# A new table of due times for the software-pipelined period of a two-layer graph network on one core

## The chip, the core and the metric

The kernel runs on one core of one Trainium2 chip. The metric is the device time of one launch in microseconds (us). The kernel before took 772.05 us as the median of three runs (771.89 to 772.5). Names of engines: PE is the matrix engine (its weight loads are shown apart as PEld), DVE the vector engine, ACT the scalar engine, POOL the general engine, SP the engine whose queue issues most DMAs.

## What is computed

There are 128 graphs of 128 nodes with 64 features. An edge exists where `adj > 0`. Two layers follow each other, each with a residual and a layer norm:

```python
# layer 0, F = 64, H = 192
mask = adj > 0
h   = relu((x @ W1a)[:, :, None, :] + (x[:, :, None, :] - x[:, None, :, :]) @ W1b + b1)
hm  = einsum('bjkh,bjk->bjh', h, mask)
x   = layernorm(x + hm @ W2 + deg[..., None] * b2)
# layer 1, H = 128, out 64
agg = einsum('bmn,bnd->bmd', adj, x)
x   = layernorm(x + elu(elu(agg @ V1 + c1) @ V2 + c2) @ V3 + c3)
```

The costly part is `hm`: for each edge a vector of 192 is formed, rectified and summed over the neighbours of a node.

## The kernel before

The graphs are worked off in 64 pairs. For one pair p the steps are these, with the line on which their PE instructions stand:

- `prepare`: DVE makes the mask and the degrees (L545), POOL copies the degrees (L552, L553), PE spreads them over the partitions (step "spread", three products, issued by `stationary` on L246 or L248), DVE ranks the nodes by degree (L568) and builds the permutation (L575).
- `sort_mask`: PE sorts the mask and turns the permutation round (step "sort", four products through `stationary`), ACT copies the results (mtp L659, permT L661), PE forms the prefix sums (step "prefix", one product of 256 columns through `stationary`), ACT copies them (vp L668), DVE builds nine one-hot tables (oh, L675).
- `sort_x` and `project_a`: PE sorts x (L592), ACT copies it (xsT L596), PE multiplies by the weights (step "proja", L606), ACT adds the bias (aj, L613), POOL and DVE form a correction (L620, the PE step "short" on L626 and L629, L635, L642).
- `turn` and `project_c`: PE transposes adj and x (L690, L691), ACT copies them (turned, L695), PE multiplies by the weights (step "projc", L708 and L711), ACT, DVE and POOL split the product into three bf16 parts (L718, L722, L725, L727).
- nine `unit`s: for a block of nodes ACT fills a PSUM bank with aj (L910), PE adds the gathered neighbours by 18 matmuls over the one-hot table (L920), DVE sums absolute values (L930). The blocks have 162, 66, 168, 112, 168, 154, 169, 154 and 170 columns.
- `finish`: POOL subtracts the correction (L842), PE projects (step "proj", L847 and L851), ACT copies (ys, L855), PE unsorts (L864), then the norm, PE aggregates (step "agg", L871), ACT copies (agg, L875), PE, ACT and DVE make the two hidden layers (steps "hid1" L880, "hid2" L886; elu on L791, L794, L797), PE makes the last layer (step "last", L891 and L893), then the norm and the store.

PE holds its array in one of three shapes: whole (128 rows by 128 columns), in two halves of 64 columns (the units, "short", sortx L592, "agg"), and in two halves of 64 rows (L708). `stationary` (L242 to L248) issues a product in two instructions of 64 columns each when the array stands in column halves at that point of the plan, and in one instruction of 128 columns otherwise.

The order of everything is written out at build time. The class `Flow` keeps a model clock for each engine and a list of threads, one for each of the pieces above. A thread yields its next step with an engine, a cost in us and the events that it needs. The table `DUE` gives each step of each thread a time relative to `ROUND * p`, with `ROUND = 11.1651`. While `under_way` is set, which holds from the first unit until 14 units before the last, `run` takes from the steps whose events are already planned the one with the smallest due time, whatever its readiness:

```python
            if self.under_way:
                t, th = min(ready, key=lambda r: self._rank(r[1]))
```

So in the middle of the run the order within one period, on every engine, is what `DUE` says. The costs and `CHANGE`, the model's charge for leaving a PE shape, enter the times at which the model believes a bank or a value to be free, and the choice before the first unit and in the last 14. Four PSUM banks, m0 to m3, serve all steps but the units, which have four of their own, e0 to e3; a step that needs a bank takes the one that heads the list of freed banks (`self.free.pop(0)`), so the order of the steps also decides which bank each uses, and with it for whose copy it waits.

Of the kernel before, what the change touches and what calls it, by code (L numbers as in the profile page):

```python
# [47 lines left out]
def gnn_kernel(ctx: ExitStack, tc: tile.TileContext, x, adj, w1, b1, w2, b2,  # L48
# [28 lines left out]
    with ExitStack() as fast:  # L77
        loads = fast.enter_context(tc.tile_pool(name="loads", bufs=8))
        prep = fast.enter_context(tc.tile_pool(name="prep", bufs=5))
        work = fast.enter_context(tc.tile_pool(name="work", bufs=5))  # L80
        ps_e = fast.enter_context(tc.tile_pool(name="ps_e", bufs=1, space=bass.MemoryType.PSUM))
        ps_m = fast.enter_context(tc.tile_pool(name="ps_m", bufs=1, space=bass.MemoryType.PSUM))
        K = sparse(tc, locals())
# [103 lines left out]
def sparse(tc, env):  # L187
# [15 lines left out]
    AHEAD = 4  # L203

    DUE = {
        "prepare": (-42.67, -37.79, -37.67, -37.41, -37.15),
        "sort_x": (-21.11, -18.03, -15.85, -13.03, -12.9, 2.76, 2.89, 3.02, 3.14),
        "sort_mask": (-28.04, -27.66, -27.27, -15.21, -14.95, -14.31, -14.05, -13.8, -13.54,
                      -13.28, -3.02, -2.76, -2.5, -2.25),
        "turn": (-38.05, -37.92),  # L210
        "project_c": (-31.63, -29.71, -29.58, -29.45, -29.32, -17.13, -13.15),
        "finish": (12.51, 20.73, 21.24, 21.37, 21.5, 21.88, 22.01, 27.91, 28.3, 28.68, 32.02,
                   34.97, 35.1, 35.23, 41.26, 41.39, 43.95, 44.08, 46.78, 46.91, 54.48, 54.61,
                   59.48),
        "unit": [(0.06, 0.19, 0.32), (0.83, 0.96, 1.09), (0.45, 0.58, 0.71), (2.37, 2.5, 2.63),
                 (3.27, 3.4, 3.53), (4.43, 4.56, 4.68), (4.81, 4.94, 5.07), (5.33, 5.71, 6.1),
                 (7.64, 10.97, 11.1)],
    }

    def begin_thread(name, p, gen):  # L220
# [958 lines left out]
```

## Time and profile before

| | |
|---|---|
| median of three runs | 772.05 us |
| the profiled execution's own time | 772.32 us |
| its span, first to last instruction | 770.6 us |
| PE busy | 746.3 us, 97% of the span |
| DVE, ACT, POOL busy | 725.2, 705.5, 430.1 us |
| mean granted PE clock | 0.985 |
| chain that ended last, by engine | PE 94%, DVE 3%, ACT 2% |
| one period (start of L847 to the next start of L847 in the middle of the run) | 11.39 us |

Times in the profile are us unless marked ns. A row of a group names the line, the engine, the operation, the tile written and the tiles read, the shapes and the number of instructions, then the busy time, the mean ns of one, and the idle time of the engine before them with what ended it. A row of the timeline gives start, duration, engine and line; idle time before it stands in brackets. Matmuls are pipelined, so their durations overlap, and a PE that is busy all the time isn't therefore at its peak: what a step costs is read from the distance between its start and the next step's start. A float32 product stands as two matmuls and two weight loads in the trace.

### The profile page before, as it was taken

To read this page: it belongs to the slowest core of one execution; us is meant where nothing else is said; L and a number is where in the kernel's file an instruction comes from. 1 tells how busy PE (TensorE), PEld (TensorE's weight loads), DVE (VectorE), ACT (ScalarE), POOL (GpSimd) and SP (SyncE) were. 2 spreads that over 40 slices of the span, in tenths; PEclk is the share of its full clock that TensorE was granted. 3 is DMA by queue.
4 is the path that set the end of the run, shared out by engine and by line. 5 is a ranking of instruction groups with operands and counts; after the bars stand their busy time and mean duration, and the time that the engine had idled before them with its cause. 6 is when DMAs were issued, how large, how long until landed. Compare 5 with 4: busy or idle time off the path is not lost.

```text
span 770.6 us, 36007 instructions
## 1 busy us (share of the span) xinstructions
PE 746.3 (97%) x14616; PEld 679.5 (88%) x14617; DVE 725.2 (94%) x2381; ACT 705.5 (92%) x1986; POOL 430.1 (56%) x801
## 2 busy tenths in 40 slices
PE   7599999999999999999999999999999999999995
PEld 5489999999999999999999999999999999999993
DVE  6699999999999999999999999999999999999994
ACT  5479999999999999999999999999999999999984
POOL 5145565565565565556556556556555655655652
PEclk9699999999999999999999999999999999999997
DMA  4000010110110011011011011011101101100000
GB/s 123 11 3 3 17 30 17 30 31 20 27 30 23 24 31 30 16 31 30 17 30 30 17 30 31 21 26 31 30 17 30 31 16 31 31 17 19 11 10 21
DMA packets 54668, 19.70 MB, mean 26 GB/s; under 512 B 37601, under 2 KB 54497, under 8 KB 54497
## 3 DMA queue, kind: packets, MB, share of 16 engines
q1 hardware_dynamic: 53792, 17.05, 9.1%
q8 instruction: 116, 1.90, 1.0%
q14 instruction: 56, 0.45, 0.2%
q10 hardware_dynamic: 704, 0.30, 0.2%
HBM read 13.14 MB, written 4.19 MB: 22 GB/s over the span
## 4 chain that ended last, share of the span: by engine, by line
PE 94%; DVE 3%; ACT 2%; issue 0%; DMA 0%; POOL 0%; ACTq 0%; POOLq 0%; DVEq 0%
PE e L920 45%; PE m L606 6%; PE m L708 5%; PE m L847 5%; PE m L880 4%; PE m L886 4%; PE m L864 4%; PE m L893 4%; PE m L690 3%; PE m L248 2%; PE m L871 2%; PE m L592 2%; PE m L246 2%; PE m L851 1%; PE m L711 1%; PE m L691 1%
## 5 line engine op out<-in xcount | busy, mean ns | idle before, releaser
L920 PE MATMUL e<-oh,cp 128*64 128x162 bf16 (+3 forms) x10368 | 392.7, 229 | 6.2 <-DVE oh L675 5.2
L920 PEld LDWEIGHTS <-cp 128*64 128x64 bf16 x10368 | 356.9, 110 | 15.3 <-issue 6.9
L930 DVE TENSOR_REDUCE sums<-e 128x54 f32<-128x486 f32 (+8 forms) x576 | 327.1, 609 | 16.7 <-PE m L629 9.9
L910 ACT COPY e<-aj 128x504 f32<-128x504 f32 (+6 forms) x576 | 293.3, 540 | 9.5 <-DVE sums L930 8.9
L749 POOL TENSOR_SCALAR ve<-st 128x2 f32<-128x2 f32 x126 | 24.1, 191 | 254.1 <-DVE st L742 246.9
L675 DVE TENSOR_TENSOR oh<-vp,slotc 128x308 bf16<-128x308 bf16 (+6 forms) x576 | 137.3, 314 | 0.8 <-ACT vp L668 0.6
L750 POOL TENSOR_TENSOR rs<-ve,mhalf 128x2 f32<-128x2 f32 x126 | 87.8, 696 | 10.5
L727 POOL TENSOR_TENSOR cp<-r,cp 128x512 bf16<-128x512 f32 x64 | 74.4, 1162 | 18.6 <-ACT cp L725 18.6
L642 POOL TENSOR_TENSOR corr<-ea,sa 128x384 f32<-128x384 f32 x64 | 64.2, 1003 | 32.8 <-DVE ea L635 32.8
L842 POOL TENSOR_TENSOR hm<-sums,corr 128x384 f32<-128x384 f32 x63 | 63.1, 1002 | 5.8 <-DVE sums L930 5.8
L620 POOL TENSOR_TENSOR sa<-aj,srow 128x384 f32<-128x384 f32 x64 | 65.4, 1021 | 0.0
L797 DVE SCALAR_TENSOR_TENSOR h<-m,cc,e 128x256 f32<-128x256 f32 x128 | 60.8, 475 | 3.8 <-ACT e L794 3.6
L791 ACT ACTIVATE r<-m,cc 128x256 f32<-128x256 f32 x128 | 61.3, 479 | 2.4 <-PE m L886 2.4
L606 PEld LDWEIGHTS m<-xsT,wad 128*128 128x128 f32 x384 | 48.3, 193 | 13.0 <-ACT turned L695 11.8
L613 ACT ACTIVATE aj<-m,b1c 128x128 f32<-128x128 f32 x192 | 57.2, 386 | 2.3 <-PE m L606 2.3
L606 PE MATMUL m<-xsT,wad 128*128 128x128 f32 x384 | 58.4, 289 | 0.6 <-DVE r L722 0.6
L794 ACT ACTIVATE e<-r 128x256 f32<-128x256 f32 x128 | 53.3, 418 | 2.0
L847 PE MATMUL m<-w2d,hm 128*128 128x128 f32 x384 | 53.4, 276 | 0.0
L722 DVE TENSOR_TENSOR r<-m,cp 128x256 f32<-128x256 f32 x128 | 47.8, 415 | 2.8 <-ACT cp L718 2.8
L771 ACT ACTIVATE x<-y,nb,rs 128x64 f32<-128x64 f32 x126 | 48.9, 439 | 1.4 <-POOL nb L753 1.4
L847 PEld LDWEIGHTS m<-w2d,hm 128*128 128x128 f32 x384 | 48.1, 192 | 0.1
L708 PE MATMUL m<-wc,turned 64*128 64x256 f32 x256 | 46.3, 436 | 0.9 <-DVE r L722 0.9
(159 smaller groups left out, 1350.5 us busy)
## 6 DMA issues: line engine op xcount, KB each, us to landing
adj<-in_adj_dram SPq DMA_DIRECT2D x64, 128.0 KB, 2.4
xx<-in_x_dram SPq DMA_DIRECT2D x64, 64.0 KB, 2.2
out_dram<-o SPq DMA_DIRECT2D x64, 64.0 KB, 1.6
w1s<-in_L_gnn_W_dram ACTq DMA_DIRECT2D x2, 96.0 KB, 2.8
w2s<-in_L_gnn_W_dram ACTq DMA_DIRECT2D x2, 48.0 KB, 2.7
v2s<-in_L_gnn_W_dram SPq DMA_DIRECT2D x1, 64.0 KB, 2.3
v1d<-in_L_gnn_W_dram SPq DMA_DIRECT2D x2, 32.0 KB, 2.0
rows<-in_L_gnn_b_dram SPq DMA_DIRECT2D x1, 64.0 KB, 4.8
```

Of the source, the lines that this page charges most:

```text
L606: nc.tensor.matmul(aps[:, c * N:(c + 1) * N], wad[:, c, :], xsT, start=True, stop=True)
L620: evs, = yield ("POOL PORT", 1.0, [have] + made("srow"), 0, lambda: nc.gpsimd.tensor_mul(sa, aj, srow))
L642: ev, = yield ("POOL PORT", 1.05, [ev, evs], 0, lambda: nc.gpsimd.tensor_sub(corr, ea, sa))
L675: lambda: nc.vector.tensor_tensor(oh[:, :, c].rearrange("p b (s w) -> p b s w", w=w), vp[:, :, p0:p1].rearrange("p b (o w) -> p b o w", o= ...
L708: nc.tensor.matmul(cps[s][:, :cols], d["turned"][k, 2, :], wc[k, :], start=True, stop=False)
L727: lambda: nc.gpsimd.tensor_sub(cp[:, 2], r1, cp[:, 1]))
L750: nc.gpsimd.tensor_tensor(rs, ve, mhalf, op=OP.pow)
L842: lambda: (nc.vector if late else nc.gpsimd).tensor_sub(hm, d["sums"], d["corr"]))
L847: nc.tensor.matmul(yb[:, :2 * O], hm[:, c, :], flat(w2d[:, c]), start=(c == 0), stop=False)
L910: lambda: nc.scalar.copy(e.rearrange("p (c s w) -> p c s w", c=3, w=w), d["aj"][:, :, p0:p1].rearrange("p c (o w) -> p c o w", o=1) .to_br ...
L920: nc.tensor.matmul(e[s * HB:(s + 1) * HB, c * n:(c + 1) * n], cp[:, k, s, c * HB:(c + 1) * HB], oh[:, s, base:base + n], start=False, stop ...
L930: nc.vector.tensor_reduce(d["sums"][:, :, p0:p1], e.rearrange("p (c s w) -> p c w s", c=3, w=w), AX.X, OP.add, apply_absolute_value=True)
```

## The change

Only the table `DUE` changes; every step, its cost in the plan, `ROUND`, `CHANGE`, the pools and the banks stay as they are. The new due times come from a plan in which leaving a PE step for another kind of matmul was charged by its time in a trace; that plan isn't part of the kernel, only its table is.

```diff
     DUE = {
-        "prepare": (-42.67, -37.79, -37.67, -37.41, -37.15),
-        "sort_x": (-21.11, -18.03, -15.85, -13.03, -12.9, 2.76, 2.89, 3.02, 3.14),
-        "sort_mask": (-28.04, -27.66, -27.27, -15.21, -14.95, -14.31, -14.05, -13.8, -13.54,
-                      -13.28, -3.02, -2.76, -2.5, -2.25),
-        "turn": (-38.05, -37.92),
-        "project_c": (-31.63, -29.71, -29.58, -29.45, -29.32, -17.13, -13.15),
-        "finish": (12.51, 20.73, 21.24, 21.37, 21.5, 21.88, 22.01, 27.91, 28.3, 28.68, 32.02,
-                   34.97, 35.1, 35.23, 41.26, 41.39, 43.95, 44.08, 46.78, 46.91, 54.48, 54.61,
-                   59.48),
-        "unit": [(0.06, 0.19, 0.32), (0.83, 0.96, 1.09), (0.45, 0.58, 0.71), (2.37, 2.5, 2.63),
-                 (3.27, 3.4, 3.53), (4.43, 4.56, 4.68), (4.81, 4.94, 5.07), (5.33, 5.71, 6.1),
-                 (7.64, 10.97, 11.1)],
+        "prepare": (-43.06, -42.93, -39.21, -39.08, -35.87),
+        "sort_x": (-26.76, -10.46, -10.33, -3.14, -3.02, 2.5, 2.63, 2.76, 2.89),
+        "sort_mask": (-26.12, -25.99, -25.86, -23.42, -23.29, -23.16, -13.67, -13.28, -13.03,
+                      -12.77, -2.63, -2.25, -1.99, -1.73),
+        "turn": (-36.9, -36.77),
+        "project_c": (-32.15, -29.32, -29.2, -29.07, -28.94, -4.17, -4.04),
+        "finish": (12.64, 19.44, 19.57, 21.62, 21.75, 21.88, 22.01, 28.04, 28.17, 29.2, 33.56,
+                   33.69, 33.82, 34.71, 43.31, 43.44, 44.47, 44.6, 46.52, 46.65, 48.06, 48.19,
+                   59.87),
+        "unit": [(-1.48, 0.96, 1.09), (2.12, 2.25, 2.37), (3.02, 3.14, 3.27), (3.66, 3.79, 3.91),
+                 (4.68, 4.81, 4.94), (5.07, 5.2, 5.33), (5.97, 6.1, 6.22), (6.35, 6.48, 6.61),
+                 (7.25, 11.61, 11.74)],
     }
```

What it makes of the order was read from the two built programs. The number of instructions on DVE, ACT, POOL and SP is the same, and SP's order is the same. On PE the number of products is the same, but more of them are issued in two halves: 842 matmuls on L246 in place of 498, and 91 on L248 in place of 263. One period on PE in the middle of the run, from "proj" on, with the units by their columns, the bank in brackets, and the array's shape ahead of each stretch:

```
before
whole    proj(m2) hid1(m1) unsort(m3)
columns  170 162 168 66
rows     projc(m2,m3)
whole    last(m0)
columns  112 short(m1) 168 sortx(m0) 154 169 sort(m1) 154 agg(m2)
whole    turn(m3) spread(m1) prefix(m2) hid2(m0) proja(m3)

after
whole    proj(m2) hid2(m0) prefix(m3) unsort(m2) hid1(m1)
columns  170 sortx(m3) 162
rows     projc(m2,m0)
whole    last(m3)
columns  66 short(m1) 168 112 168 154 spread(m3) agg(m1) 169 154 sort(m2)
whole    turn(m0) proja(m1)
```

On ACT, within a period, the copy of turned (L695) is followed at once by aj, ys and the fill of a unit, and not by vp; xsT (L596) follows the elu of both layers and not the copy of agg. On DVE the ranks (L568) stand between two sums over units, and the permutation (L575) among the one-hot tables and not ahead of them. On POOL sa (L620) follows the small degree copies (L552, L553), and the two norms stand apart.

## Prediction

> **What bounds the kernel now.** I read the page first, then the span cut into its stages, then one period instruction by instruction.
>
> ```profile
> PE 746.3 (97%) x14616; PEld 679.5 (88%) x14617; DVE 725.2 (94%) x2381; ACT 705.5 (92%) x1986; POOL 430.1 (56%) x801
> PEclk9699999999999999999999999999999999999997
> ```
>
> The stretches of the span (length, then busy us of PE, PEld, DVE, ACT, POOL, granted clock):
>
> ```profile
> 25.40:50.60 25.20, 17.84 (x363) 15.92 (x363) 20.39 (x68) 15.16 (x41) 5.58 (x8) 0.83 0.01 3
> 72.10:721.10 649.00, 649.00 (x12993) 595.40 (x12992) 630.23 (x2046) 625.11 (x1765) 376.35 (x680) 1.00 0.10 25
> 721.10:770.60 49.50, 40.09 (x711) 35.86 (x709) 37.03 (x118) 34.27 (x96) 23.20 (x42) 0.90 0.06 14
> ```
>
> From 72.1 to 721.1 PE is never idle: 57 equal periods of 649.0/57 = 11.386 us, 84% of the span. So the period is a sum of PE steps, each from its start to the next one's start. But a wait can hide in this: a matmul's recorded duration runs on while its weights are still missing. Such waits show as a first pass that is longer than its sisters. The timeline around the whole-array steps:
>
> ```profile
> 389.44 0.14 PEld L691 LDWEIGHTS m<-ident,xx 128*128 128x128 f32 x1
> 389.56 0.27 ACT L596 COPY xsT<-m 128x128 f32<-128x128 f32 x1
> 389.77 0.10 PEld L248 LDWEIGHTS <-prefix 128*128 128x128 bf16 x1
> 389.82 0.27 PE L248 MATMUL m<-mtp,prefix 128*128 128x256 bf16 x1
> 389.86 0.48 ACT L695 COPY turned<-m 128x384 f32<-128x384 f32 x1
> 389.88 0.30 PEld L886 LDWEIGHTS m<-h,v2s 128*128 128x128 f32 x2
> 389.93 0.43 PE L886 MATMUL m<-h,v2s 128*128 128x256 f32 x1
> 390.20 0.38 PE L886 MATMUL m<-h,v2s 128*128 128x256 f32 x1
> 390.38 0.30 PEld L606 LDWEIGHTS m<-xsT,wad 128*128 128x128 f32 x2 [0.21 <-ACT turned L695]
> 390.42 0.35 PE L606 MATMUL m<-xsT,wad 128*128 128x128 f32 x1
> ...
> 392.00 0.36 PE L880 MATMUL m<-agg,v1p 128*128 128x128 f32 x1
> 392.20 0.27 ACT L855 COPY ys<-m 128x128 f32<-128x128 f32 x1
> 392.53 0.32 PE L864 MATMUL m<-ys,permT 128*128 128x64 f32 x1
> ```
>
> Three loads come just after an ACT copy ends: L886 (hid2, bank m0) at 389.88, after xsT has left m0 at 389.83; L606 (proja, m3) at 390.38, after turned has left m3 at 390.34; L864 (unsort) 0.05 after ys is there. Their first passes take 432, 346 and 315 ns where later ones take 378, 275 and 276:
>
> ```profile
> L886 PE MATMUL m<-h,v2s x128: 378/432/797, 70.9 to 761.7; 128*128 128x256 f32 x128
> L606 PE MATMUL m<-xsT,wad x384: 274/275/527, 15.0 to 731.0; 128*128 128x128 f32 x192
> ```
>
> The excess is 54 + 71 + 39 = 164 ns in each period, in which PE is counted busy. A cross-check without the wait is the early round whose L606 starts right behind "prefix": 49.90 to L847 at 50.56, 0.67 us, against 390.42 to 391.16, 0.74 us.
>
> **What the Trainium skill says.** "TensorE: Matmul & The Clock Gate", section "LDWEIGHTS (loading the stationary operand)", prices a load by its columns, 128/1.2 = 107 ns as an estimate; float32 loads here follow each other by 0.11 us, which agrees. Its table at the top says that loads are pulled ahead of running matmuls; L606 at 49.79 beside "prefix" agrees, and a load that waits for a bank (above) loses just this. "TensorEngine Tiling (Array Packing)", "Key Properties", says that changing the tiling mode drains the engine: "agg" (column halves) starts at 388.94, its passes need 0.22, and turn (whole) starts at 389.27, so the drain costs 0.1 us. Part 1 of the first page says that the clock halves when PE is idle; the 6 in the second slice of PEclk agrees.
>
> **The change, part by part.**
>
> *Switches of shape.* A period before has whole, columns, rows, whole, columns, whole: five. After it has the same five. At 0.1 us each this is neither gain nor loss; only the neighbours change (rows after 162 and not 66, whole after the bf16 "sort" and not after "agg").
>
> *Spread in halves.* Before, three whole products take 389.66 to 389.82 = 0.17 us. After, six half products: "sort" has eight of the same size in 388.09 to 388.31 = 0.22, so 6 x 0.028 = 0.17. Nothing.
>
> *The whole-array steps.* Before, from "prefix" on: prefix 0.11, hid2 0.49, proja 0.74, proj 0.84, hid1 0.53, unsort 0.58 (with the drain) = 3.29. After: proja behind turn, in bank m1 and so not waiting for the copy of turned: 6 x 0.112 = 0.67. proj 0.84. hid2 now follows the 64-column bf16 passes of proj, which hide only 0.03 of its 0.11 load: that exposure is what hid1 shows today (356 against 275 ns), 0.08; 0.08 + 2 x 0.215 = 0.51. prefix 0.11, and its 256 columns hide unsort's load. unsort 4 x 0.112 = 0.45. hid1 3 x 0.112 + 0.205 with the drain = 0.54. Sum 3.12. The difference, 0.165 us, is the same as the three waits: the exposure behind proj only changes its owner. 57 periods x 0.165 = 9.4 us.
>
> *What becomes late next.* unsort still needs ys: today it comes 0.55 us after proj's last pass, and in between stand hid2's 0.51 and a bit, so its margin is about nil; I take no loss, at worst 0.05. proj takes bank m2 from sort, so it waits for permT: the copies end 1.1 us after sort starts (388.09 to 389.21), and turn and proja give it 0.22 + 0.15 + 0.38 + 0.67 = 1.4 us; the margin of 0.3 is used up if ACT is at the fill of a unit (0.53) when sort ends: from nothing to 0.2 lost, I take nothing. prefix now waits for vp and a bank behind hid2, with mtp made 1.5 us ahead. On DVE, nine one-hots, nine sums and the rest need 13.5 us of durations in a period, of which back-to-back ones overlap by 0.08 (nine one-hots of mean 0.314 take 2.14 us together): 32 instructions, so 10.9 us. In a period of 11.22 this leaves 0.3. ACT and POOL have more. SP's order is the same, loads land periods ahead of use.
>
> *The start.* Before the first unit the order also changes. Today the first unit stands from 25.76 to 30.68 behind DVE's chain of constants (L508 at 24.14 to L366 at 28.7) and nine one-hots (2.15 us); the chain starts when PE has run L504 and L505, which stand behind two runs of projc. In the new order one of these runs comes after L505, but the split of its product (L722, two of 0.41) stands inside the chain. I work out L504 some 2.5 us sooner, of which the wait for that projc (at half clock 1.8 us, and copies) takes half back: 1.2 gained. Between 30.68 and 50.56 PE also idles: 1.17 (DVE r), 0.56, 0.42 and 0.29 before units, more inside L606. The new order puts the second pair's projc and sortx elsewhere; I take 1.8 of it as saved. So 3.0, bounds 0 and 5.5 (the upper one with the full clock coming back sooner; it is 0.83 on average in that stretch).
>
> *The end.* The last store was due 59.48 after its period's start and is due 59.87; the last 14 units run in a free order in both. I take 0, bounds -1.5 and +1.5.
>
> Sum against the profiled execution: 772.3 - 9.4 - 3.0 = 759.9; the median of the runs is 0.3 below that execution, so **759.6 us**.
>
> **The rivals.**
>
> *A, the forecast:* the three waits go, nothing takes their place, the start is shorter. 756 to 763 us.
>
> *B, the waits change places:* permT before proj, or ys before unsort, or the fill of a unit. For it speaks that the new margins are 0 to 0.3 us. With 0.1 lost per period, 57 x 0.1 = 5.7: 765 us, range 763 to 770.
>
> *C, DVE becomes the bound:* its need is 10.9 us and it is idle 0.5 today. If its new order leaves the same idle time, the period stays at 11.39; with no gain at the start either, 772. Against it: what it waits for today is mostly PE, which comes sooner.
>
> *D, slower:* the elu behind hid2. projc takes bank m0 from hid2, so it waits for h2 (L797). From hid2's last pass (390.20) to the end of h2 takes 3.85 us today (the same step a period earlier: r at 379.63, e at 380.97, h at 382.18 to 382.65). After, PE reaches projc's load 0.22 + 0.11 + 0.45 + 0.54 + 0.69 + 0.22 + 0.73 = 2.96 later. If ACT and DVE took as long as now, each period would lose 0.89 - 0.165 = 0.72, 41 us in all: 813 us. It decides from 3.1 us on. Against it: on ACT r now stands one unit fill behind ys, and e behind vp alone, and on DVE h2 directly behind y and its statistics: 0.38 + 0.49 + 0.26 + 0.42 + 0.48 and some 0.4 of queueing, 2.4 us.
>
> *E, the change does nothing at run time:* a charge in a plan isn't executed, only the order is. But the built order does differ, as shown, on four engines.
>
> **How the numbers follow.** A 0.75, B 0.15, C and E 0.04, D 0.06. Within 0.2% is about what a measurement of this kernel can tell from no change (1.5 us). A and B are faster, save for a small part of B's far end; D is slower. Faster 0.91, same 0.04, slower 0.05. The range takes A whole and the nearer half of B: 756 to 766.
>
> **What would show it.** Right: in the middle a period of 11.2 us; first passes of L606 and L864 near 275 ns; of L886 near 460 and of L880 near 275; no idle PE there. Wrong: a period of 11.3 or more with PE idle or a long first pass at L847, L864 or L708; DVE busy throughout. The start is right if L847 first runs near 47.5 and not 50.56. The least sure term is the start; the forecast falls as a whole only if the period doesn't shorten.

## The result, and the profile after

The kernel after takes 759.41 us (median of four runs, 758.81 to 759.95); the kernel before, in the same comparison, 772.27 us (771.89 to 772.51). The ratio is 0.983, with a 95% interval of 0.982 to 0.985. The profiled execution of after took 759.95 us and its span is 758.2 us.

The page of after, first the engines' busy time, then the clock in 40 slices:

```profile
PE 736.3 (97%) x14788; PEld 672.4 (89%) x14789; DVE 722.5 (95%) x2381; ACT 705.7 (93%) x1986; POOL 432.4 (57%) x801
PEclk9799999999999999999999999999999999999998
```

PE's busy time fell by 10.0 us and its share stayed at 97%. The stretches of the span (length, busy us of PE, PEld, DVE, ACT, POOL, clock):

```profile
21.80:46.50 24.70, 18.67 (x374) 16.44 (x375) 20.22 (x65) 15.25 (x39) 6.57 (x8) 0.79 0.01 2
67.40:695.00 627.60, 627.60 (x12907) 577.88 (x12908) 617.28 (x2011) 612.51 (x1731) 371.37 (x671) 1.00 0.11 26
695.00:758.20 63.20, 53.68 (x980) 48.65 (x974) 49.27 (x152) 48.26 (x135) 31.05 (x53) 0.94 0.06 13
```

PE is still never idle in the middle, as before; the periods are shorter all the same. The whole-array stretch of one period on PE:

```profile
369.87 0.44 PE L690 MATMUL m<-ident,adj 128*128 128x128 f32 x2
370.15 0.27 PE L691 MATMUL m<-ident,xx 128*128 128x128 f32 x1
370.26 0.83 PE L606 MATMUL m<-xsT,wad 128*128 128x128 f32 x6
370.93 0.83 PE L847 MATMUL m<-w2d,hm 128*128 128x128 f32 x6
371.60 0.34 PE L851 MATMUL m<-cp,mtp 128*128 128x64 bf16 x6
371.77 0.68 PE L886 MATMUL m<-h,v2s 128*128 128x256 f32 x2
372.29 0.27 PE L248 MATMUL m<-mtp,prefix 128*128 128x256 bf16 x1
372.40 0.56 PE L864 MATMUL m<-ys,permT 128*128 128x64 f32 x4
372.79 0.66 PE L880 MATMUL m<-agg,v1p 128*128 128x128 f32 x4
```

The same period's passes by line, as min/median/max ns. The first pass is the longest one in the rows of L886 and L880 and the shortest one in that of L864:

```profile
L606 PE MATMUL m<-xsT,wad x6: 275/275/275, 370.3 to 370.8; 128*128 128x128 f32 x6
L886 PE MATMUL m<-h,v2s x2: 379/421/463, 371.8 to 372.1; 128*128 128x256 f32 x2
L864 PE MATMUL m<-ys,permT x4: 222/275/275, 372.4 to 372.7; 128*128 128x64 f32 x4
L880 PE MATMUL m<-agg,v1p x4: 275/275/328, 372.8 to 373.2; 128*128 128x128 f32 x4
```

proja's first pass is down from 346 to 275 ns, unsort's from 315 to 222 and hid1's from 356 to 328; hid2's is 463 for 432. Cut at the starts of L847, the gain of 12.4 us in the span lies here:

| stretch of the span | before | after | gain | forecast |
|---|---|---|---|---|
| to the first L847 | 50.57 | 46.48 | 4.08 | 3.0, with the next row |
| from the first to the third pair's L847 | 21.55 | 20.97 | 0.58 | |
| from the third to the 58th, 55 periods | 626.71 | 618.20 | 8.51 | 9.4 in 57 periods |
| from the 58th to the end | 71.77 | 72.56 | -0.80 | 0 |

A period is 11.395 before and 11.240 after, a gain of 0.155 us. The whole-array steps, from each start to the next step's start, in us:

| | prefix | hid2 | proja | proj | hid1 | unsort | sum |
|---|---|---|---|---|---|---|---|
| before | 0.109 | 0.486 | 0.740 | 0.844 | 0.528 | 0.580 | 3.287 |
| after | 0.109 | 0.515 | 0.670 | 0.844 | 0.593 | 0.393 | 3.124 |

The difference is 0.163 us; the rest of the period, in columns and rows, is 0.008 longer. "spread" in six half products takes 0.167 us, the same as in three whole ones.

### The profile page after: what moved, and what is told of

The parts are those of the page before. It is cut to its first block, busy times and chain, and to the rows that moved or that the text cites. A ratio compares the mean times of both kernels' runs of the same rounds, so it can differ in the third digit from the quotient of the medians.

```text
span 758.2 us, 36118 instructions
## 1 busy us (share of the span) xinstructions
PE 736.3 (97%) x14788; PEld 672.4 (89%) x14789; DVE 722.5 (95%) x2381; ACT 705.7 (93%) x1986; POOL 432.4 (57%) x801
## 4 chain that ended last, share of the span: by engine, by line
PE 95%; DVE 2%; ACT 1%; DMA 1%; issue 0%; POOL 0%; POOLq 0%; SPq 0%; DVEq 0%; ACTq 0%
PE e L920 46%; PE m L606 6%; PE m L708 5%; PE m L847 5%; PE m L886 4%; PE m L880 4%; PE m L893 4%; PE m L864 3%; PE m L246 3%; PE m L690 3%; PE m L592 2%; PE m L871 2%; PE m L851 1%; PE m L711 1%; PE m L248 1%; PE m L691 1%
## 5 line engine op out<-in xcount | busy, mean ns | idle before, releaser
L930 DVE TENSOR_REDUCE sums<-e 128x54 f32<-128x486 f32 (+8 forms) x576 | 334.4, 608 | 10.2 <-PE e L920 4.6
L675 DVE TENSOR_TENSOR oh<-vp,slotc 128x308 bf16<-128x308 bf16 (+6 forms) x576 | 148.9, 315 | 4.8 <-ACT vp L668 1.3
L620 POOL TENSOR_TENSOR sa<-aj,srow 128x384 f32<-128x384 f32 x64 | 64.3, 1005 | 1.0 <-ACT aj L613 1.0
L606 PE MATMUL m<-xsT,wad 128*128 128x128 f32 x384 | 53.7, 276 | 0.0
L847 PE MATMUL m<-w2d,hm 128*128 128x128 f32 x384 | 53.5, 276 | 0.0
L722 DVE TENSOR_TENSOR r<-m,cp 128x256 f32<-128x256 f32 x128 | 47.7, 414 | 1.6 <-ACT cp L718 1.6
L718 ACT CAST cp<-m 128x256 bf16<-128x256 f32 x128 | 40.3, 366 | 8.8 <-PE m L711 8.8
L847 PEld LDWEIGHTS m<-w2d,hm 128*128 128x128 f32 x384 | 48.0, 192 | 0.3 <-POOL hm L842 0.3
```

The lines of the kernel that those rows point to most:

```text
L606: nc.tensor.matmul(aps[:, c * N:(c + 1) * N], wad[:, c, :], xsT, start=True, stop=True)
L620: evs, = yield ("POOL PORT", 1.0, [have] + made("srow"), 0, lambda: nc.gpsimd.tensor_mul(sa, aj, srow))
L675: lambda: nc.vector.tensor_tensor(oh[:, :, c].rearrange("p b (s w) -> p b s w", w=w), vp[:, :, p0:p1].rearrange("p b (o w) -> p b o w", o= ...
L847: nc.tensor.matmul(yb[:, :2 * O], hm[:, c, :], flat(w2d[:, c]), start=(c == 0), stop=False)
L930: nc.vector.tensor_reduce(d["sums"][:, :, p0:p1], e.rearrange("p (c s w) -> p c w s", c=3, w=w), AX.X, OP.add, apply_absolute_value=True)
```

## The experiments

Two theories stood against each other. Mine: in the middle PE's steps wait for ACT, which gives back a bank or a value by copying it, and the order decides how long; these waits hide in first passes. The rival is what the change's words say: a PE step costs according to the kind of its neighbour, and the new order has cheaper neighbours. For the start there were two as well: the chain of constants comes sooner, or prefix and the one-hots of the first pairs do. A third question was DVE, at 95%.

Each edit changes due times, unless said otherwise. All the kernels are timed against the kernel before, whose median in the three comparisons was 772.16, 771.88 and 771.80 us; "period" is the mean over 55 periods in the middle.

### One wait of the three is taken away

```diff
-        "sort_x": (-21.11, -18.03, -15.85, -13.03, ...
+        "sort_x": (-21.11, -18.03, -16.6, -13.03, ...
```

> Kernel before with one due time changed: the copy of xsT out of its bank (L596) is due 0.75 earlier, nothing else. The banks that rotate then fall otherwise, and hid2 (L886) no longer waits for xsT's copy. If the three excesses of first passes (54, 71 and 39 ns) add up, as my sum took them, hid2's 54 goes: period 11.39 - 0.054 = 11.34, and 57 x 0.054 = 3 us in all, 769. If hid2's wait lies inside the time that proja waits anyway for the copy of turned (L695), proja's first pass grows by what hid2's loses, to about 400 ns from 346, hid2's falls to 378, and the period and the time stay at 11.39 and 772. If only the neighbours' kinds count (no wait matters), first passes are noise and nothing changes either: 772.

Measured: 771.63 us, ratio 0.9996 (0.9987 to 1.0005), period 11.395 as before. The passes of hid2 and proja in one of its periods:

```profile
L886 PE MATMUL m<-h,v2s x2: 379/380/382, 388.1 to 388.3; 128*128 128x256 f32 x2
L606 PE MATMUL m<-xsT,wad x6: 275/275/377, 388.5 to 389.2; 128*128 128x128 f32 x6
```

hid2 lost its excess, and proja's first pass grew from 346 to 377 ns; from step to step hid2 fell by 31 ns and proja rose by 32. The timeline says what holds proja:

```profile
388.01 0.48 ACT L695 COPY turned<-m 128x384 f32<-128x384 f32 x1 [0.19 <-PE m L691]
388.54 0.74 PEld L606 LDWEIGHTS m<-xsT,wad 128*128 128x128 f32 x6 [0.26 <-ACT turned L695]
```

The load starts 0.05 us after the copy of turned has ended. So an excess isn't what its removal alone is worth: hid2's wait lay inside proja's.

### Spread alone is moved

```diff
-        "prepare": (-42.67, -37.79, -37.67, -37.41, -37.15),
+        "prepare": (-42.67, -38.9, -38.75, -37.41, -37.15),
```

> Kernel before with only the three bf16 products of spread moved (two due times), from between turn and prefix to between the last fill in columns and agg. The order of the steps else is the same. If waits for copies set the pace: spread's 0.17 us stood between turn and hid2 and covered part of the copies of xsT and turned; these copies end no sooner, so hid2 and proja wait about 0.17 us longer in their first passes, and spread costs its own time before agg: period 11.39 + 0.15 to 0.2, time 780 to 784. If the kinds of neighbours set it: spread leaves whole for whole neighbours and comes between columns and columns, at most two more switches of 0.1 us: also slower by up to 0.2, but then with first passes of hid2 and proja as before (432 and 346 ns). If neither matters: 772.

Measured: 781.73 us, ratio 1.012 (1.010 to 1.014), period 11.564, longer by 0.169. At its new place spread costs nothing beyond its own time (0.165 us, and agg 0.340 after it where it had 0.335). At its old place three starts slipped: turn to prefix by 0.056 us, prefix to hid2 by 0.060, hid2 to proja by 0.050, together 0.166, which is spread's own time. Of the first passes hid2's grew, to 483 ns, and proja's stayed at 346; the loss stands in the distances between the starts, and what ends them are copies. The copies of this stretch on ACT, and the loads that wait for them:

```profile
381.82 0.27 ACT L875 COPY agg<-m 128x128 f32<-128x128 f32 x1 [0.36 <-PE m L871]
...
381.99 0.27 ACT L596 COPY xsT<-m 128x128 f32<-128x128 f32 x1
382.14 0.27 PE L248 MATMUL m<-mtp,prefix 128*128 128x256 bf16 x1
382.28 0.48 ACT L695 COPY turned<-m 128x384 f32<-128x384 f32 x1
382.31 0.30 PEld L886 LDWEIGHTS m<-h,v2s 128*128 128x128 f32 x2 [0.23 <-ACT xsT L596]
...
382.81 0.74 PEld L606 LDWEIGHTS m<-xsT,wad 128*128 128x128 f32 x6 [0.21 <-ACT turned L695]
```

hid2's and proja's loads each start 0.05 us after a copy's end (382.26, 382.76), and prefix's product 0.05 after agg's (382.09). Before, spread's time was filled waiting time, and so it was free there. The neighbours' kinds speak for no such loss at turn and hid2, which are whole and have whole neighbours in both.

### proja alone is moved ahead

```diff
-        "sort_x": (-21.11, -18.03, -15.85, -13.03, ...
+        "sort_x": (-21.11, -18.03, -16.6, -14.8, ...
```

> Kernel before with one part of the new order alone: proja (L606) is moved ahead of hid2 (L886), behind prefix, and its xsT copied 0.75 earlier (two due times). All kinds of neighbours stay the same (whole before and after). If waits add up and only those of the moved steps count, hid2's 54 and proja's 71 ns go: period 11.27, 765. If a wait changes place: on ACT the elu's r (L791) now comes 0.67 later and stands ahead of aj (0.89) and ys (0.27), so ys is 0.2 to 0.5 us late for unsort (L864), whose first pass grows by that: period 11.45 to 11.75, 776 to 792. If only kinds of neighbours count: 772.

Measured: 782.12 us, ratio 1.013 (1.011 to 1.015), period 11.564. proja takes 0.670 and hid2 0.434 us, so both waits went, 0.122 us. But unsort stands 0.286 us later behind hid1. ACT's lines, one behind the other, and the load that follows them:

```profile
383.68 0.47 ACT L791 ACTIVATE r<-m,cc 128x256 f32<-128x256 f32 x1
384.05 0.88 ACT L613 ACTIVATE aj<-m,b1c 128x128 f32<-128x128 f32 x3
384.80 0.28 ACT L855 COPY ys<-m 128x128 f32<-128x128 f32 x1
385.13 0.52 PEld L864 LDWEIGHTS m<-ys,permT 128*128 128x128 f32 x4 [0.31 <-ACT ys L855]
```

In ACT's order of this plan hid2's r now waits for hid2 behind proja, aj stands behind r, and ys behind aj. A wait changed its place, and grew.

### unsort directly behind proj, in the kernel after

```diff
-        "finish": (12.64, 19.44, 19.57, 21.62, 21.75, ...
+        "finish": (12.64, 19.44, 19.57, 20.9, 21.75, ...
```

> Kernel after with one due time changed: unsort (L864) directly behind proj, ahead of hid2 and prefix. The kinds of neighbours stay (whole, whole, whole). My theory: ys comes 0.55 us after proj's last pass whatever stands there, so unsort waits about 0.5 us where hid2 and prefix covered it: period 11.24 + 0.5 = 11.75, 57 x 0.5 = 28 us, 787, all in L864's first passes or as idle time before them. If kinds of neighbours explain the gain: 759.5, no change from after.

Measured: 792.81 us, ratio 1.027 (1.025 to 1.029), period 11.780, longer than after by 0.540. From proj to unsort it takes 1.363 us, where proj alone takes 0.844. Again ACT's lines and the load that follows them:

```profile
387.04 0.88 ACT L613 ACTIVATE aj<-m,b1c 128x128 f32<-128x128 f32 x3
387.88 0.27 ACT L855 COPY ys<-m 128x128 f32<-128x128 f32 x1
388.20 0.52 PEld L864 LDWEIGHTS m<-ys,permT 128*128 128x128 f32 x4 [0.48 <-ACT ys L855]
```

Every neighbour is whole, as in after, and the loss is the wait for ys. Of the total's 33 us the middle explains 55 x 0.54 = 30; the start and the end took the rest.

### hid2 back between turn and proja, in the kernel after

```diff
-                   33.69, 33.82, 34.71, 43.31, 43.44, 44.47, ...
+                   33.69, 33.82, 34.71, 41.45, 41.58, 44.47, ...
```

> Kernel after with one part undone: hid2 is put back between turn and proja (two due times), prefix stays behind proj. If waits set the pace, undoing it costs far more than the 0.15 us a period that the whole change won: prefix meets the bank of aj (0.2 to 0.3 us, as where prefix was moved alone), and ys is ready 0.55 us after proj's last pass with only prefix's 0.11 in front of unsort, with r of hid2 ahead of aj on ACT: another 0.2 to 0.3. Period 11.6 to 11.75, 780 to 789. If kinds of neighbours count: 759.5, since hid2 keeps whole neighbours.

Measured: 789.79 us, ratio 1.023 (1.021 to 1.025), period 11.762, a little over what I expected. proja takes 0.089 more (a first pass that waits again), from proj to prefix 0.292 more than proj's 0.844 (the bank of aj), prefix to unsort 0.227 for 0.109 and unsort 0.495 for 0.393 (ys); hid2 itself is 0.081 shorter. The part undone loses 0.52 us a period, more than three times what the whole change won.

### prefix alone is moved behind proj, in the kernel before

```diff
-        "sort_mask": (-28.04, -27.66, -27.27, -15.21, -14.95, -14.31, ...
+        "sort_mask": (-28.04, -27.66, -27.27, -12.72, -12.6, -12.55, ...
```

> Kernel before with one part of the new order alone: prefix (L248 with mtp, and its copy vp) is moved from between turn and hid2 to behind proj (three due times). Middle: hid2 and proja stand 0.11 us closer to turn, whose copies end no sooner, so hid2 and proja win nothing; hid1 and unsort come behind proj's last 64 columns and prefix. If only kinds count: 11.39. If banks count: prefix and hid1 take the banks that proja's aj copy (L613, 0.89 us for three) gives back late, so hid1 or prefix waits some 0.1 to 0.3 us: 11.45 to 11.6, 776 to 784. Start: by my account the first unit stands behind the constants chain, which is ahead of the first one-hots on DVE in this order as well, with ea (0.54) no longer in front of it; then L847 first runs at about 49 to 50.5. If the place of prefix and of the one-hots in the first pairs is what shortens the start, it runs at 46.5 to 47.5 as after.

Measured: 784.8 us, ratio 1.017 (1.014 to 1.020), period 11.597. The period lies where the account by banks had it: hid1 now waits for aj's bank, with 0.292 us from prefix to hid1 and 0.612 for hid1 where it took 0.528. Two things came otherwise than I wrote. In the middle proja lost its wait (0.668 us; the banks fall otherwise when prefix goes). And at the start L847 first runs at 45.73 us, sooner than in after: see below.

### prefix and hid2 exchanged, in the kernel after

```diff
-        "sort_mask": (-26.12, -25.99, -25.86, -23.42, -23.29, -23.16, ...
+        "sort_mask": (-26.12, -25.99, -25.86, -23.9, -23.8, -23.72, ...
```

> Kernel after with one pair of neighbours exchanged: prefix ahead of hid2 behind proj (three due times). Kinds and shapes stay the same, all are whole. Reading the passes alone it should gain: the bf16 prefix needs only a short load behind proj's 64 columns, and its 256 columns hide hid2's first load, so the 0.08 us that hid2 pays today go: 11.16, 755. If banks decide: one step comes 0.43 us sooner behind proj than today, and takes the bank that the copies of aj (L613) give back: aj's three copies follow proja's passes and end about 0.9 to 1.1 us after proja's last pass, proj takes 0.84 of that, so the one that has this bank waits 0.1 to 0.3 us: 11.35 to 11.5, 766 to 774.

Measured: 770.97 us, ratio 0.999 (0.998 to 1.000), period 11.444. The load that should have been hidden waits for a bank:

```profile
375.60 0.88 ACT L613 ACTIVATE aj<-m,b1c 128x128 f32<-128x128 f32 x3
...
376.53 0.30 PEld L886 LDWEIGHTS m<-h,v2s 128*128 128x128 f32 x2 [0.22 <-ACT aj L613]
```

prefix, at 376.24, takes the bank that turned has long left, and the second step takes aj's, which comes back at 376.48. In after it is the other way round: aj's bank comes back at 372.01 and prefix's product starts at 372.29, so it is in time. This exchange of two neighbours costs 0.204 us, more than the whole gain.

### The old order in the first eight pairs, the new one after

Both tables stand in the kernel; threads of the first eight pairs take their due times from the old one:

```diff
-        flow.start(ROUND * p, DUE[name], gen)
+        flow.start(ROUND * p, (DUE if p < 8 else DUE2)[name], gen)
```

> The due times of before for the threads of the first eight pairs, those of after for all later pairs and for the end. It separates the start from the middle. If the middle's gain depends on the order in a period alone: L847 first at 49.5 to 50.6 as before, periods of 11.24 once the change-over is through (from about the twelfth), a loss of some us in the change-over itself, 763 to 768 in all. If the middle's gain needs the early start (a lead that PE keeps over the copies): periods stay near 11.39 and the time near 772.

Measured: 772.47 us, ratio 1.001 (1.000 to 1.002). L847 first runs at 50.77 us, and from the tenth period on every period is 11.24. So start and middle are independent gains. My total was wrong: the change-over took 6.4 us more than nine periods of before do (107.7 us from the first L847 to the tenth, 101.3 before), where I had thought of "some us", and it ate most of the middle's gain of 48 x 0.155 = 7.4; the stretch from the 58th L847 to the end took another 1.3 more than before.

### Work added on DVE, in the kernel after

One memset of 128x128 in each period, and in a second kernel two of 128x384:

```diff
+            if i == 4:
+                nc.vector.memset(filler[:, :128], 0.0)
```

> Kernel after with one piece of DVE work added in each period that nobody waits for: a memset of 128x128 f32 behind the reduce of the fifth unit, about 0.12 to 0.17 us by the row of the 128x384 memset (378 ns). If DVE has the slack of about 0.3 us in a period that I worked out (10.9 of 11.24): no change, 11.24 and 759 to 760.5. If DVE is the bound (rival C): each period grows by the whole of it, 11.36 to 11.4, 766 to 769.

> Kernel after with two pieces of DVE work added in each period that nobody waits for: memsets of 128x384 f32 (378 ns each by their row, about 0.3 where they follow another instruction) behind the reduces of the second and sixth unit, 0.6 to 0.76 us together. If DVE has about 0.3 us of slack in 11.24: the period becomes 11.24 + 0.3 to 0.45, 11.54 to 11.7, 776 to 786, and DVE is then never idle. If DVE is the bound: 11.84 to 12, 793 to 802. If DVE has more slack than I worked out: under 11.4.

Measured: with the one memset (165 ns) 760.26 us and a period of 11.240: no change. With the two (378 ns each; the next instruction starts 0.30 us after them, so 0.61 together) 775.89 us and 11.523: 0.283 longer. That is just under the range expected. DVE's slack is 0.61 - 0.28 = 0.33 us in a period. In the second kernel (whose lines stand two lower) no PE idle time shows in the middle; the groups of projc and proj are what grew, in 52 periods here and 53 in after:

```profile
L706 PE MATMUL m<-wc,turned 64*128 64x256 f32 x208 | 46.9, 428 | 0.0
L845 PE MATMUL m<-w2d,hm 128*128 128x128 f32 x312 | 47.7, 289 | 0.0
```

And in after:

```profile
L708 PE MATMUL m<-wc,turned 64*128 64x256 f32 x212 | 37.2, 428 | 0.0
L847 PE MATMUL m<-w2d,hm 128*128 128x128 f32 x323 | 44.9, 275 | 0.0
```

From start to start projc takes 0.901 us for 0.703 and proj 0.929 for 0.844, which is the whole 0.283. One of projc's two banks is hid2's, given back by h2 on DVE: h2 ends at 405.51, and projc's second row half starts at 405.57, 0.21 us behind the first, where both start within 0.01 us in after. proj doesn't wait for hm, which is ready 4.9 us before proj's load. It waits for the bank that the copy of permT gives back. That copy ends a run of ACT without a break, and the run begins with the fill of a unit that waits 0.28 us for a sum on DVE:

```profile
406.14 0.45 ACT L908 COPY e<-aj 128x336 f32<-128x336 f32 x1 [0.28 <-DVE sums L928]
...
412.26 0.39 ACT L659 COPY permT<-m 128x256 f32<-128x256 f32 x1
412.70 0.41 PEld L845 LDWEIGHTS m<-w2d,hm 128*128 128x128 f32 x3
```

The load starts 0.05 us after that copy's end (412.65). So the work added on DVE comes to proj by way of ACT.

### The chain of constants alone is started sooner

In the kernel before, and in a second kernel in the kernel after:

```diff
-    flow.start(ROUND * -0.5, [0.0], consts_late())
+    flow.start(ROUND * -1.5, [0.0], consts_late())
```

> Kernel before with one number changed: the thread of the last constants (L504, L505 and the DVE chain L508 to L366) starts a period earlier (-1.5 for -0.5 periods). In the profile of before L504 runs at 22.98 behind two runs of projc. My account of the start: this chain sets the first unit, so with L504 1.5 to 3 us sooner the second matmul of the first unit comes at 27.5 to 29.2 instead of 30.68, L847 first at 47.5 to 49.3 instead of 50.56, and the total falls by 1.3 to 3 us, to 769 to 770.6; the middle stays at 11.39. If the start's gain comes from where prefix and the one-hots of the first pairs stand: L847 first at 50 to 50.8, 772.

> Kernel after with the same one number changed. In its profile the chain of constants still has the first unit wait from 21.9 to 27.7. If the chain sets the start: first unit up to 1.5 us sooner, 758 to 759. If something else does by now (cp of the first pair, which waits for a copy on ACT, is in the middle of the chain): no change, 759.5. Middle at 11.24 in either case.

Measured: in before 770.08 us, ratio 0.998 (0.997 to 0.999), L847 first at 49.00, period unchanged. The first unit's second product runs at 29.30 where it ran at 30.68. In after 757.51 us, a little under the 758 to 759 expected, ratio to before 0.981 (0.980 to 0.983), L847 first at 43.57, period 11.240. That is the fastest of all kernels here; its interval overlaps that of after, so the 1.9 us between them are likely but not settled.

The start of before and of after on DVE, the first and the last instruction of the chain and the one-hots behind it. Before:

```profile
24.14 0.15 DVE L508 TENSOR_TENSOR cc<-cc,m 128x1 f32<-128x1 f32 x1 [0.88 <-PE m L505]
28.52 0.19 DVE L366 COPY rowp<-low 1x128 bf16<-1x128 bf16 x1
28.72 2.15 DVE L675 TENSOR_TENSOR oh<-vp,slotc 128x324 bf16<-128x324 bf16 x9
```

After:

```profile
20.35 0.15 DVE L508 TENSOR_TENSOR cc<-cc,m 128x1 f32<-128x1 f32 x1 [0.54 <-ACT e L910]
22.36 0.76 DVE L722 TENSOR_TENSOR r<-m,cp 128x256 f32<-128x256 f32 x2 [1.33 <-ACT cp L718]
26.03 0.18 DVE L366 COPY rowp<-low 1x128 bf16<-1x128 bf16 x1
26.23 1.92 DVE L675 TENSOR_TENSOR oh<-vp,slotc 128x132 bf16<-128x132 bf16 x8
```

The chain starts 3.8 us sooner, loses 1.3 to projc's split (L722) in its midst, and ends 2.5 us sooner. The clock has part in it. The stretch from 20.4 to 23.9 (length, busy times, clock, then DMA's share and GB/s), in before:

```profile
20.40:23.90 3.50, 2.63 (x11) 1.82 (x11) 1.76 (x6) 1.16 (x3) 0.56 (x1) 0.50 0.02 3
```

In after:

```profile
20.40:23.90 3.50, 1.53 (x7) 0.59 (x7) 2.00 (x11) 1.93 (x6) 0.24 (x1) 1.00 0.00 0
```

Before, L504 ran at 22.98, behind projc, at half clock; after, L504 runs at 19.60, and L505 and projc are through at full clock too. Moving prefix alone gave 4.8 us at the first L847; there L504 runs at 19.94, ahead of the half clock, and the one-hots follow the chain at once (25.30). Moving the constants alone gave 1.6, although L504 runs at 20.11 there, nearly as early. Its chain ends at 25.44, 3.3 us sooner than in before, but then other work of DVE stands ahead of the nine one-hots of the first units:

```profile
25.46 1.31 DVE L675 TENSOR_TENSOR oh<-vp,slotc 128x324 bf16<-128x324 bf16 x5
26.68 0.75 DVE L722 TENSOR_TENSOR r<-m,cp 128x256 f32<-128x256 f32 x2
27.35 2.13 DVE L675 TENSOR_TENSOR oh<-vp,slotc 128x324 bf16<-128x324 bf16 x9
```

So both rivals hold a part: the chain started sooner wins something by itself, 1.7 us in the medians, but an early L504 isn't enough for the rest. In the two kernels with the larger gain the one-hots follow the chain at once (25.30 with prefix moved, 26.23 in after), and that is a matter of the order in the first pairs. The share of each in the 4.1 us isn't settled: seven kernels with the new start order have L847 first at 43.6 to 47.6 us, six with the old one (prefix moved alone not counted) at 48.7 to 50.8. Each of these starts is one execution, and in the three comparisons the executions of the kernel before alone take 770.6 to 772.8 us.

## Why the prediction was right, point by point

*The total* was right (759.6 for 759.41), but with three errors that cancel, so that it came this close is in part luck: the middle was forecast 0.9 us too good, the start 1.7 too bad and the end 0.8 too good.

*The three waits.* Right, and at the places named: the first pass of proja is at 275 ns and that of hid2 at 463 (forecast near 460). For unsort and hid1, both forecast near 275, the first passes are 222 and 328: 0.05 us changed sides between these neighbours, and the two steps together were forecast at 0.99 us and took 0.986. The sum of whole-array steps was forecast at 3.12 us and is 3.124. The period before was read as 11.386 us, because 721.1 is not a start of L847; from start to start it is 11.395. A period gained 0.155 and not 0.165: 0.163 by these steps, less the 0.008 by which the rest grew. That, and two periods that belong to the start and the end, is the 0.9 us in the middle. What the working didn't say is that the three excesses may not be taken one by one: with hid2's removed the period stayed the same, and with hid2's and proja's removed it grew. They add up here because the new order breaks all three at once and puts nothing in their place.

*Switches of shape and spread in halves.* Nothing, as forecast: 0.167 us for spread, and 0.008 us in all of columns and rows. The rival that kinds of neighbours explain the gain falls: in five kernels (proja, prefix or unsort moved, prefix and hid2 exchanged, hid2 put back) every moved step stayed among whole-array steps, with as many or fewer changes between float32 and bf16, and the period grew by 0.17 to 0.54 us. Such a price exists: hid2 is 0.081 us shorter where it doesn't follow proj's bf16 passes. But whatever float32 step follows them pays it, in both orders.

*What becomes late next.* ys was forecast with a margin of about nil: it is ready at 372.24 (the copy starts at 371.97 and takes 0.27), and unsort's load starts at 372.29. It is in time because hid2 and prefix stand ahead of unsort: directly behind proj, unsort was 0.52 us late. That hid2's r doesn't stand ahead of aj on ACT helps too: where it did, with proja moved alone, unsort came 0.286 us later. For permT the margin was put at 0.3 us; its copy ends at 370.63 and proj's load starts at 370.82, 0.19 later, and no time is lost. DVE's slack was worked out as 0.3 and measured as 0.33, so rival C was sized rightly and did not come about. For rival D the end of h2 was put at 2.4 us behind hid2's last pass and comes after 2.59 (372.07 to 374.66), projc's load at 2.96 and comes at 2.95 (375.02): a margin of 0.36, and no wait. The kernel with more DVE work shows that these two margins, of h2 and of permT, are the next to go.

*The start.* The mechanism (constants sooner) was right and its size too small: the term that failed is "1.2 gained" up to the first unit. L504 came 3.4 us sooner and not 2.5, ahead of the half clock, so that the chain starts 3.8 us sooner. projc's split took 1.3 back, about as forecast; the one-hots behind the chain let the first unit come another 0.5 sooner. Its second product is 2.97 us sooner in all. What followed it, forecast as 1.8, was 1.7 us in all (to the third L847).

*The end.* Forecast as 0, lost 0.8, inside the bound of 1.5. The kernel with one wait taken away, whose period is that of before, also takes 72.56 us from the 58th L847 to the end (one execution each), so the end can differ as much with a single due time changed. Why it does wasn't tried.

## What to carry to other kernels

Before an order is changed, list for each matrix step the bank and the value that it takes, and whose copy releases them and what stands ahead of that copy on its engine: a PE that is 100% busy can hide those waits in first passes. Don't price such a wait by its excess alone, and don't judge a new order by its parts: here proja or prefix moved alone lost 0.17 and 0.20 us a period, and the whole won 0.155. Work of which the place was free may have been filling a wait, as spread did, and can cost its full time when it leaves.

## What was not expected of the hardware

- A wait of PE need not show as idle time. With two more DVE memsets PE's record in the middle shows 598.50 us busy in 598.50, as before, and yet a period takes 0.283 us more. In proj the wait is a longer first pass (358 ns for 275, 0.085 us in the period). In projc no pass is longer: its two row halves start 0.21 us apart where they started together, and the pass of the first covers the wait of the second (0.198 us).
- PE idles from 25.76 to 30.68 before and from 22.1 to 27.7 after, and the clock is at half until 34.1 in both, though PE restarted 3 us sooner in after. In the kernel after with its constants sooner PE restarts at 25.72, and from 30 to 34.1 the clock is full. So the restart alone doesn't say when the full clock comes back. What the fourteen traces show is that the stretch at half clock in the start always lasts a whole multiple of 3.413 us: 6.83 in two kernels, 10.24 in nine, 13.65 in two (before is one) and 17.07 in one. So a small shift in the start may bring one such step more or less at half clock.
